# Attention: summing both halves of the older block behind all four heads' scores in the middle slots of a group

## The chip, the cores and the metric

The kernel runs on one core of one Trainium2 chip. The time is that of the whole program on the device, in microseconds (us), the median of several runs. Five engines work side by side: TensorE (PE) multiplies matrices, VectorE (DVE), ScalarE (ACT) and GpSimd (POOL) do the rest, and SyncE (SP) issues transfers. PEld is the loading of weights into TensorE.

## The reference

The input is 2048 tokens of 256 features. Two macaron layers follow one another; each is half a feed-forward network, causal attention with 16 heads of 16 features, and the other half of the feed-forward network, every one behind a layer norm:

```
x = x + 0.5 * ffn0(ln(x));  x = x + attn0(ln(x));  x = x + 0.5 * ffn0(ln(x))
x = x + 0.5 * ffn1(ln(x));  x = x + attn1(ln(x));  x = x + 0.5 * ffn1(ln(x))

q, k, v = heads(x @ W_qkv)                       # 16 heads, 16 features each
s = q @ k.T / 4 (+ position bias in layer 0, rotary q and k in layer 1), masked where key > query
y = softmax(s) @ v;  out = y @ W_o
```

ffn0 has ternary weights and an RMS norm; ffn1 keeps the two largest of each four hidden values. The change touches attention alone, in both layers.

## The kernel before

**Tiling.** Tokens are cut into four chunks c = 0 to 3 of 512 queries (CH), the 16 heads into four quartets g. A group n = 4c + g is one chunk of queries with one quartet of heads, so there are 16 groups per layer. The keys that a group may see are cut into blocks kb of 128 keys, 4(c + 1) of them; T = 4 is the number of blocks in a chunk. A pair (n, kb) is a slot. A layer has 160 slots (16 in c = 0, 32 in c = 1, 48 in c = 2, 64 in c = 3), and `slots` lists them in order (line 833).

**Work of a slot.** For its own block the slot forms the scores of four heads, keys on partitions, in two pairs: `st_pair` (line 725, matmuls at line 733, output `pst`) for heads 2 and 3 (hp = 1) and then heads 0 and 1 (hp = 0). A pair takes two PSUM banks, from a pool of two such pairs. `exp_pair` (line 746, ScalarE, line 753) turns each pair into `pT` in SBUF, which has five buffers. Softmax needs the maximum of every query's scores beforehand, so beside this the slot works ahead for a later group: a "unit" (n, t, kc) of `mx_unit` (line 663) forms, for each of four heads, the scores of 128 queries against 512 keys (matmul `pq`, line 671) and VectorE reduces each to a maximum (`mx`, line 682). A `pq` takes one PSUM bank from a pool of three, `ps_one`. The banks go round, so the fourth `pq` of a unit takes the bank of the first and waits until VectorE has read it. The list `maxima` says which units belong to which slot; slots of groups 0 to 14 with kb <= cT have at least one, and those of the last group have none.

**Sums.** `av_part` (line 759, matmul at line 768, output `pav`) multiplies an older block's `pT` with the values and adds into one PSUM bank `acc` for the whole group. The bank holds the four heads in four strips of 32 partitions, and the work is split into two halves of the query columns, part 0 and part 1. One part of a block with 512 columns is four matmuls of 32 weight columns x 256, one per head; they are f32, and the trace shows two records for each, so eight. Blocks wait for their sums in the deque `unsummed`; `sums(i, part)` (line 929) sums everything up to that part of slot i's block.

**Order.** The order of the instructions on PE, VectorE, ScalarE and GpSimd is that of the Python code; nothing reorders it. In a slot i with a unit (lines 949 to 954) it is: scores of heads 2 and 3, maxima of heads 0 and 1, exponentials, part 1 of block i - 2; then scores of heads 0 and 1, maxima of heads 2 and 3, exponentials, part 0 of block i - 1. In a slot without a unit (lines 955 to 964) both score pairs come first and then both parts of block i - 1. Behind that come the other units of the slot, what has fallen due (`run_due`: turning maxima, the output projection at line 809), and one step of preparing the next chunk (`prep_qk`, `prep_v`) or of a layer norm. Loads of q and k are issued on SP three slots ahead (`load_to(i + 3)`).

Of the kernel before, what the change touches and what calls it, by code (L numbers as in the profile page):

```python
# [31 lines left out]
T = CH // P  # L32
# [14 lines left out]
def macaron_kernel(ctx: ExitStack, tc: tile.TileContext, a, out):  # L47
# [139 lines left out]
    def draw(work):  # L187
        while work and next(work[0], "end") == "end":
            work.popleft()

    def pull():

        for work in list(background)[:2]:
            if next(work, "end") == "end":
                background.remove(work)
# [294 lines left out]
    def attention(layer, following):  # L490
# [9 lines left out]
        with ExitStack() as st:  # L500
# [91 lines left out]
            def prep_v(c):  # L592
                ready(c)
                for t in range(0, T, 2):
                    pp = ps_one(f"pv{layer}_{c}_{t}").rearrange("p (t f) -> p t f", t=2)
                    for i in range(2):
                        for dc in range(DC):
                            nc.tensor.matmul(  # L598
                                pp[:, i, :],
                                lhsT=xns[c][:, dc, (t + i) * P : (t + i + 1) * P],  # L600
                                rhs=wqkv[:, dc, 2 * E : 3 * E],
                                start=dc == 0,
                                stop=dc == DC - 1,
                            )
                    for i in range(2):
                        vs = va[c][:, t + i, 0 : H * VW].rearrange("p (h d) -> p h d", d=VW)[:, :, 0:D]
                        pv = pp[:, i, :].rearrange("p (h d) -> p h d", d=D)
                        if layer == 0:
                            nc.scalar.copy(vs, pv)
                        else:  # L610
                            nc.vector.tensor_tensor(
                                vs, pv, b_v.rearrange("p (h d) -> p h d", d=D), ALU.add
                            )
                    if t + 2 == T:
                        done.add(("v", c))
                    yield
# [108 lines left out]
            def st_pair(n, kb, hp, apart=False):  # L725

                c, g = divmod(n, G)
                kc, t = divmod(kb, T)
                lo = t * P if kc == c else 0
                pair, ps = banks(f"pst{layer}_{n}_{kb}_{hp}", apart)  # L730
                for i in range(2):
                    hh = 2 * hp + i
                    nc.tensor.matmul(  # L733
                        ps[i][:, lo:CH],
                        lhsT=ks[n, kc][0:rows, hh, t * P : (t + 1) * P],
                        rhs=qs[n][0:rows, hh, lo:CH],
                        start=True,
                        stop=kc < c,
                    )
                    if kc == c:  # L740
                        nc.tensor.matmul(  # L741
                            ps[i][:, lo : lo + P], lhsT=ident_b, rhs=mask_kq, start=False, stop=True
                        )
                return pair, ps

            def exp_pair(n, kb, hp, scores):
                pair, ps = scores
                c, g = divmod(n, G)
                kc, t = divmod(kb, T)
                lo = t * P if kc == c else 0  # L750
                pT = ap.tile([P, 2, CH], F32, tag="pT", bufs=5, name=f"pT{layer}_{n}_{kb}_{hp}")
                if pair is not None:
                    nc.scalar.activation(pT[:, :, lo:CH], pair[:, :, lo:CH], AF.Exp, scale=0.25)  # L753
                else:
                    for i in range(2):
                        nc.scalar.activation(pT[:, i, lo:CH], ps[i][:, lo:CH], AF.Exp, scale=0.25)
                return pT

            def av_part(n, kb, pTs, part):
                c, g = divmod(n, G)  # L760
                kc, t = divmod(kb, T)
                lo = t * P if kc == c else 0
                mid = (lo + CH) // 2 if CH - lo > CH // 2 else CH
                a, b = ((lo, mid), (mid, CH))[part]
                if a < b:
                    for hh in range(4):
                        v0 = (4 * g + hh) * VW
                        nc.tensor.matmul(  # L768
                            acc[hh * SLOT : (hh + 1) * SLOT, a:b],
                            lhsT=va[kc][:, t, v0 : v0 + SLOT],  # L770
                            rhs=pTs[hh // 2][:, hh % 2, a:b],
                            start=kb == 0 and part == 0,
                            stop=kb == (c + 1) * T - 1,
                            skip_group_check=True,
                        )
                if part == 0 and kc == c:
                    divide(n, t)
# [89 lines left out]
            def run_due(all_of=False):  # L867
                while True:
                    due = [x for x in later if all_of or x[0] <= now[0]]
                    if not due:  # L870
                        return
                    later.remove(due[0])
                    due[0][1](*due[0][2])
# [3 lines left out]
            def step():  # L877
                draw(preps)

            def need(*what):  # L880
                while what not in done:
                    assert preps, what
                    step()
# [6 lines left out]
            def mx_next(unit, heads):  # L890
                n, t, kc = unit
                mx_unit(n, t, kc, heads)
                if 3 in heads:
                    left[n] -= 1
                    if not left[n]:
                        mx_end(n)
                        at(1, mx_turn, n)
# [8 lines left out]
            def load_to(slot):  # L906
                while uses and uses[0][1] <= slot:
                    load(*uses.popleft()[0])
# [12 lines left out]
            def turned(n):  # L921
                if n % 2 == 1:
                    c, q = divmod(n // 2, G // 2)
                    at(2, turn_back, c, q)
                    if q == G // 2 - 1:
                        for dc in range(DC):
                            at(3 + dc, output, c, dc)

            def sums(i, part):

                while unsummed and unsummed[0][::2] <= (i, part):
                    _, unit, p = unsummed.popleft()
                    n, kb, _ = unit
                    need("v", kb // T)
                    av_part(*unit, p)
                    if p == 1 and kb == (n // G + 1) * T - 1:
                        turned(n)

            for i, (n, kb) in enumerate(slots):
                c = n // G  # L940
                if kb == 0 and n % G == 0 and 0 < c < NCH - 1:

                    preps.extend((prep_qk(c + 1, "k"), prep_qk(c + 1, "q"), prep_v(c + 1)))
                if n not in turned_max:
                    run_due(all_of=True)
                load_to(i + 3)
                units = maxima.get(i, [])
                pTs = [None, None]
                if units:
                    for hp in (1, 0):  # L950
                        ps = st_pair(n, kb, hp)
                        mx_next(units[0], (2 - 2 * hp, 3 - 2 * hp))
                        pTs[hp] = exp_pair(n, kb, hp, ps)
                        sums(i - 2 + (hp == 0), hp)
                else:


                    both = []
                    for hp in (1, 0):
                        both.append(st_pair(n, kb, hp, pairs[0] % 3 == 2))  # L960
                        pairs[0] += 1
                    for hp, ps in zip((1, 0), both):
                        pTs[hp] = exp_pair(n, kb, hp, ps)
                    sums(i - 1, 1)
                unsummed.extend((i, (n, kb, pTs), part) for part in range(2))
                for unit in units[1:]:
                    mx_next(unit, (0, 1, 2, 3))
                run_due()
                if preps and (c <= 1 or i % 2):
                    step()  # L970
                    if c == 0 and i % 2:
                        draw(background)
                else:
                    pull()
                now[0] += 1
# [37 lines left out]
    def begin(layer, following):  # L1013
        att = attention(layer, following)
        begun[:] = att, next(att)
# [149 lines left out]
```

## Time and profile before

| | us |
|---|---|
| median of three runs | 1952.8 (1952.1 to 1952.8) |
| profiled execution | 1957.7 |
| its span, first to last instruction | 1955.7 |
| PE busy | 1761.4 (90% of the span) |
| DVE busy | 1361.6 (70%) |
| ACT busy | 894.2 (46%) |
| POOL busy | 458.4 (23%) |
| attention of layer 0 | about 267 to 787 of the span, PE busy 499.6 of 521 |
| attention of layer 1 | about 1203 to 1764, PE busy 517.1 of 561 |

A timeline row gives start, length, engine, line, operation, output<-inputs, shape and how many instructions were merged; brackets hold the idle time of the engine before it and what ended it. Matmuls are pipelined: one of 512 columns is shown some 0.38 us long, while the next starts 0.22 us later. So on PE the distance between starts is what counts, not the length of a row.

### The profile page before, as it was taken

What the parts mean: (1) busy time and instruction counts of PE and PEld (TensorE: products, weight loads), DVE (VectorE), ACT (ScalarE), POOL (GpSimd) and SP (SyncE); (2) the same over time, 40 slices, a digit from 0 to 9 for tenths busy, and PEclk for the clock granted to TensorE, in tenths of its full rate; (3) what the DMA queues carried; (4) which work ended last, traced back from release to release, by engine and by line L of the source; (5) the groups of instructions that cost most, each with busy time, mean ns of one, the idle gap of its engine ahead of it and who ended that gap; (6) DMA issues with size and microseconds to landing.
All of it is one profiled execution on the core that took longest, in us unless ns stands there. A gap on an engine that the chain in (4) does not pass through costs nothing. (4 is left out here: it accounts for less than half of the span.)

```text
span 1955.7 us, 26994 instructions
## 1 busy us (share of the span) xinstructions
PE 1761.4 (90%) x10684; PEld 726.5 (37%) x10684; DVE 1361.6 (70%) x2384; ACT 894.2 (46%) x1112; POOL 458.4 (23%) x418
## 2 busy tenths in 40 slices
PE   5699789999999999789999876898999999998997
PEld 1233344433433333333444333433333333333443
DVE  7866377787788883666575655868877888825664
ACT  4343254555555668334422312445555656673220
POOL 3455321101000000455453432211111000003422
PEclk9799899999999999989999986999999999999999
DMA  4000252213211000200000115222122110000000
GB/s 129 1 1 33 82 148 83 73 54 102 62 45 46 28 28 2 73 1 0 1 11 0 54 61 158 82 73 92 52 69 86 43 43 26 18 1 0 11 11 22
DMA packets 50510, 93.10 MB, mean 48 GB/s; under 512 B 5424, under 2 KB 33072, under 8 KB 50128
## 3 DMA queue, kind: packets, MB, share of 16 engines
q1 hardware_dynamic: 49296, 89.28, 14.8%
q10 hardware_dynamic: 1088, 2.10, 0.3%
q8 instruction: 84, 1.38, 0.3%
q14 instruction: 42, 0.34, 0.1%
HBM read 59.51 MB, written 27.26 MB: 44 GB/s over the span
## 5 line engine op out<-in xcount | busy, mean ns | idle before, releaser
L682 DVE TENSOR_REDUCE mx<-pq 128x1 f32<-128x512 f32 (+3 forms) x1280 | 708.6, 603 | 158.5 <-PE pq L679 91.2
L753 ACT ACTIVATE pT<-pst 128x1024 f32<-128x1024 f32 (+3 forms) x614 | 542.6, 896 | 334.9 <-PE pst L733 196.8
L671 PE MATMUL pq<-k,q 105*128 105x512 bf16 (+7 forms) x1280 | 378.8, 353 | 74.7 <-DVE mx L682 52.3
L733 PE MATMUL pst<-q,k 99*128 99x512 bf16 (+7 forms) x1280 | 357.7, 354 | 5.1 <-ACT pT L753 4.2
L768 PE MATMUL pav<-pT,va 128*32 128x256 f32 (+1 forms) x4608 | 352.4, 382 | 5.2 <-DVE yt L789 5.0
L281 PE MATMUL pg_f<-xn,wgu 128*128 128x512 f32 x512 | 229.8, 602 | 11.5 <-DVE hr_f L318 11.5
L794 POOL TENSOR_TENSOR zt<-yt,rd 128x64 f32<-128x64 f32 x128 | 38.4, 300 | 795.2 <-DVE rd L793 795.1
L733 PEld LDWEIGHTS <-k 105*128 105x128 bf16 (+1 forms) x1280 | 101.5, 98 | 254.1 <-issue 218.4
L317 ACT ACTIVATE sl_f<-pg_f 128x512 f32<-128x512 f32 x128 | 76.0, 594 | 251.8 <-PE pg_f L281 175.0
L671 PEld LDWEIGHTS <-q 105*128 105x128 bf16 (+1 forms) x1280 | 124.5, 100 | 148.0 <-issue 44.3
L306 PE MATMUL pg_f<-xn,wgu 128*128 128x512 bf16 x512 | 156.2, 413 | 19.5 <-DVE wgu L170 6.8
L768 PEld LDWEIGHTS pav<-pT,va 128*32 128x32 f32 x4608 | 93.8, 108 | 208.7 <-issue 174.8
L281 PEld LDWEIGHTS pg_f<-xn,wgu 128*128 128x128 f32 x512 | 98.6, 193 | 136.9 <-issue 121.0
L306 PEld LDWEIGHTS <-wgu 128*128 128x128 bf16 x768 | 77.7, 101 | 166.9 <-issue 74.7
L292 PE MATMUL po_f<-h_f,wd 128*128 128x512 f32 x256 | 116.3, 608 | 17.3 <-DVE h_f L418 17.3
L340 POOL TENSOR_TENSOR ss_f<-ss_f,sq_f 128x512 f32<-128x512 f32 x56 | 91.1, 1628 | 111.5 <-ACT sq_f L339 111.3
L679 PE MATMUL pq<-mask_qk,ident_b 128*128 128x128 bf16 x512 | 107.3, 227 | 0.0
L741 PE MATMUL pst<-mask_kq,ident_b 128*128 128x128 bf16 x512 | 103.1, 222 | 0.0
L306 PE MATMUL pg_f<-xm_f,wgu 128*128 128x512 bf16 x256 | 85.3, 416 | 14.0 <-DVE xm_f L238 14.0
L318 DVE TENSOR_TENSOR h_f<-sl_f,pg_f 128x512 f32<-128x512 f32 x64 | 43.6, 682 | 76.4 <-ACT sl_f L317 76.3
L789 DVE STREAM_TRANSPOSE yt<-pav 128x128 f32<-128x128 f32 x128 | 39.8, 311 | 76.7 <-PE pav L768 76.7
L394 DVE TENSOR_TENSOR ge_f<-h_f 128x1536 bf16<-128x1536 f32 (+2 forms) x48 | 67.6, 1437 | 28.0 <-ACT h_f L387 28.0
(132 smaller groups left out, 1802.5 us busy)
## 6 DMA issues: line engine op xcount, KB each, us to landing
k<-dk SPq DMA_DIRECT2D x80, 384.0 KB
dk<-p_k SPq DMA_DIRECT2D x48, 256.0 KB
dq<-p_q SPq DMA_DIRECT2D x48, 256.0 KB
q<-dq SPq DMA_DIRECT2D x32, 384.0 KB
x<-in_xT ACTq DMA_DIRECT2D x4, 512.0 KB
raw<-in_w_gu SPq DMA_DIRECT2D x8, 256.0 KB
wgu<-in_w_gu SPq DMA_DIRECT2D x1, 2048.0 KB
cs_k<-in_cos_sin SPq DMA_DIRECT2D x4, 512.0 KB
```

What stands on the lines that cost most here:

```text
L281: nc.tensor.matmul(pg[:, half, :], lhsT=wgu[:, dc, half * F + f * P : half * F + (f + 1) * P], rhs=xn[:, dc, :], start=dc == 0, stop=dc == ...
L292: nc.tensor.matmul(po, lhsT=w[:, f, dc * P : (dc + 1) * P], rhs=h[:, f, :], start=f == 0, stop=f == FC - 1,)
L306: nc.tensor.matmul(pg[:, half, :], lhsT=wgu0[:, dc, half * F + f * P : half * F + (f + 1) * P], rhs=xp[part][:, dc, :], start=part == 0 an ...
L317: nc.scalar.activation(sl, pg[:, 0, :], AF.Silu)
L340: nc.gpsimd.tensor_tensor(ss, ss, sq, ALU.add)
L671: nc.tensor.matmul(pq, lhsT=qs[n][0:rows, hh, t * P : (t + 1) * P], rhs=ks[n, kc][0:rows, hh, 0:w], start=True, stop=kc < c,)
L679: nc.tensor.matmul(pq[:, w - P : w], lhsT=ident_b, rhs=mask_qk, start=False, stop=True)
L682: nc.vector.tensor_reduce(mxs[n][:, t, hh, kc : kc + 1], pq, AX.X, ALU.max)
L733: nc.tensor.matmul(ps[i][:, lo:CH], lhsT=ks[n, kc][0:rows, hh, t * P : (t + 1) * P], rhs=qs[n][0:rows, hh, lo:CH], start=True, stop=kc < c,)
L741: nc.tensor.matmul(ps[i][:, lo : lo + P], lhsT=ident_b, rhs=mask_kq, start=False, stop=True)
L753: nc.scalar.activation(pT[:, :, lo:CH], pair[:, :, lo:CH], AF.Exp, scale=0.25)
L768: nc.tensor.matmul(acc[hh * SLOT : (hh + 1) * SLOT, a:b], lhsT=va[kc][:, t, v0 : v0 + SLOT], rhs=pTs[hh // 2][:, hh % 2, a:b], start=kb == ...
```

## The change

In a slot that has a unit and whose block lies in the middle of its group (1 < kb < cT - 1), the two half sums between the score pairs are left out. In their place both parts of block i - 1 are summed behind the scores and maxima of all four heads. At kb = 2, the first such slot, `sums(i - 1, 1)` finds part 1 of block i - 2 still open and sums three parts; at kb = cT - 1, the first slot behind, half by half again, the first call finds nothing and the second sums part 0 alone. The condition holds for kb = 2 in c = 1, kb = 2 to 6 in c = 2 and kb = 2 to 10 in c = 3 (groups 12 to 14), 51 slots per layer. All instructions stay the same in number and shape on every engine; their order on PE changes.

```diff
                 if units:
+                    full = 1 < kb < c * T - 1
                     for hp in (1, 0):
                         ps = st_pair(n, kb, hp)
                         mx_next(units[0], (2 - 2 * hp, 3 - 2 * hp))
                         pTs[hp] = exp_pair(n, kb, hp, ps)
-                        sums(i - 2 + (hp == 0), hp)
+                        if not full:
+                            sums(i - 2 + (hp == 0), hp)
+                    if full:
+                        sums(i - 1, 1)
                 else:
```

## The prediction

> **What bounds the kernel now.** I read the page first (PE is busy 90% of the span, VectorE 70%, ScalarE 46%), then the timeline of one slot in chunk 3, where nothing else runs beside it:
>
> ```profile
> 643.06 0.61 PE L733 MATMUL pst<-q,k 105*128 105x512 bf16 x2
> 643.50 0.59 PE L671 MATMUL pq<-k,q 105*128 105x512 bf16 x2
> 643.92 1.29 DVE L682 TENSOR_REDUCE mx<-pq 128x1 f32<-128x512 f32 x2 [0.25 <-PE pq L671]
> 644.03 0.64 PE L768 MATMUL pav<-pT,va 128*32 128x256 f32 x8
> 644.60 0.61 PE L733 MATMUL pst<-q,k 105*128 105x512 bf16 x2
> 645.04 0.59 PE L671 MATMUL pq<-k,q 105*128 105x512 bf16 x2
> 645.57 0.64 PE L768 MATMUL pav<-pT,va 128*32 128x256 f32 x8
> 646.14 0.60 PE L733 MATMUL pst<-q,k 105*128 105x512 bf16 x2
> ```
>
> PE waits for nothing here (no bracket), VectorE waits for PE. A half takes 1.54 us, a slot 3.08, and 80 of the 102 slots in which the condition holds start the next slot 3.07 or 3.08 us later. So PE sets the pace and what counts is the distance between its starts. Two scores take 0.44, two `pq` 0.53 up to the sum, the sum 0.57 up to the next scores.
>
> How much of that is the switch between bf16 scores and column-tiled f32 sums? The last group, without units, sums both parts in one run (timeline, three rows of PE):
>
> ```profile
> 758.16 1.04 PE L733 MATMUL pst<-q,k 105*128 105x512 bf16 x4
> 759.31 1.07 PE L768 MATMUL pav<-pT,va 128*32 128x256 f32 x16
> 760.32 1.04 PE L733 MATMUL pst<-q,k 105*128 105x512 bf16 x4
> ```
>
> Sixteen records take 1.07 where eight take 0.64, so eight more take 0.43: two waves of four heads, 0.215 each. Four scores last 1.04 and two 0.61, so a score too takes 0.215. A half is four bf16 matmuls and two waves, 6 x 0.215 = 1.29. The rest of its 1.54 us, 0.25, is paid once for each run of sums: 0.09 ahead of it (0.53 instead of 0.44), 0.13 behind (0.57 instead of 0.44), some 0.03 inside. From start to start the run of sixteen takes 1.01 and not 2 x 0.57, which confirms it. I use 0.245, since eight slots take 24.62 us and not 24.64.
>
> The order that the change makes is already there once, at kb = 0 and 1 of chunk 3, where part 1 of a group's last block is empty and the first half has no sum (timeline, PE and DVE):
>
> ```profile
> 662.86 0.59 PE L671 MATMUL pq<-k,q 105*128 105x512 bf16 x2
> 663.28 2.48 DVE L682 TENSOR_REDUCE mx<-pq 128x1 f32<-128x512 f32 x4 [0.19 <-PE pq L671]
> 663.29 0.59 PE L733 MATMUL pst<-q,k 105*128 105x512 bf16 x2
> 663.73 0.67 PE L671 MATMUL pq<-k,q 105*128 105x512 bf16 x2
> ...
> 665.99 0.38 PE L671 MATMUL pq<-k,q 105*128 105x512 bf16 x1
> ...
> 666.83 0.38 PE L671 MATMUL pq<-k,q 105*128 105x512 bf16 x1 [0.46 <-DVE mx L682]
> ```
>
> With VectorE free (kb = 0) the second pair of `pq` lasts 0.67 instead of 0.59: the fourth waits 0.08 for the first one's bank. With VectorE behind (kb = 1) it waits 0.46.
>
> **The change, part by part.** *Switches.* In PE's order there are 540 runs of sums before and 416 after. 124 fewer: per layer two in each of the four groups of chunk 1, six in each of chunk 2, ten in each of groups 12 to 14 (the slots kb = 2 to cT - 2, and kb = cT - 1, which keeps one run). At 0.245 on the path, -30.4 us. The waves themselves only move: kb = 2 has six, kb = cT - 1 two, the others four.
>
> *The bank of the fourth `pq`.* Until now a sum and a switch lay between the second and the third `pq`, and the first bank was long free. Now the fourth `pq` waits, and behind it on PE's queue the run of sums and all the rest. Bounds: 0 (no bracket in today's halves) and 0.46 (kb = 1). I take the 0.08 of kb = 0. Its cause reads off the rows: the first maximum starts 0.42 behind its `pq`, lasts 0.69, its release reaches PE 0.05 later, at 1.16 behind the first `pq`; PE would be there at 1.08. Whether VectorE stays free: a new slot takes 12 x 0.215 + 0.245 + 0.08 = 2.91, four maxima take 2.48, so 0.4 remain. In the shortest slot (kb = cT - 1, two waves, 2.48) they just fit. 124 x 0.08 = +9.9 us.
>
> *Maxima that are late already.* A delay of VectorE that a half hid (between first and fourth `pq` there were 1.76 us) now stands on the path. Going along the timeline through the 124 slots, I noted how much later than 0.42 (0.47 in a masked unit) the first maximum starts behind its `pq`. In most it does not. The rest:
>
> ```profile
> 453.92 0.59 PE L671 MATMUL pq<-k,q 105*128 105x512 bf16 x2
> ...
> 454.30 0.69 DVE L545 TENSOR_TENSOR dn_k<-pp_k,p_k 128x512 f32<-128x512 f32 x1 [1.77 <-ACT p_k L544]
> 454.91 2.47 DVE L682 TENSOR_REDUCE mx<-pq 128x1 f32<-128x512 f32 x4
> ```
>
> Five slots of layer 0 have L545 ahead, 0.56 to 0.62 each, 2.9 together: it hangs on a projection just before the slot and stays as late. Six have the turned sums (L804), 0.29 each; five the maxima's end (L689, L694), 0.26 to 0.52, 1.8 together; one L571, 0.74; two more a layer norm, 0.52 together, and L819 makes 0.1. That is 7.8 in all. In eleven of these VectorE's queue is the reason and the slot before is changed too; its last maximum then starts 0.70 instead of 0.52 before the next slot's `pq`, which takes off 0.18 each, 2.0. I take +5.8; bounds 0, if other waits cover it, and 11.6, twice that, if the tight slots push the delay on.
>
> *Layer 1, group 5, kb = 2.* There PE waits for VectorE's preparation today; its one switch, 0.2, is not won.
>
> *Exponentials.* `pT` has five buffers. At kb = 2 the second exponential needs the buffer of block 0, whose part 1 is now summed at the slot's end: first part of the run, through at about 2.6 behind the slot's start. The exponential (1.02) then ends near 3.7 instead of 2.6. The slot lasts 14 x 0.215 + 0.245 + 0.08 = 3.34, the next one's first exponential starts at about 3.98 and its second score pair at 4.2: hidden, by 0.3. In later slots the buffers are free a slot ahead. If that cover is gone, 22 groups pay 0.3 at most, 6.6. ScalarE otherwise has 0.9 of 2.9 us idle.
>
> *Queues.* No transfer moves against its slot: SP's loads stay three slots ahead, now 8.7 us and not 9.2. GpSimd's division at line 794 belongs to blocks from cT on, which are summed half by half as before.
>
> Sum: -30.4 + 9.9 + 5.8 + 0.2 = -14.5 us. In the profiled execution that is 1955.7 - 14.5 = 1941.2 of span, 1943.2 with the 2.0 around it. The median of the runs lies 4.9 below the profiled execution, so 1952.8 - 14.5 = 1938.3.
>
> **The rivals.** *Late maxima cost nothing*, since PE has prep work to do in many of those slots: -20.3, 1932.5. Against it: that work stands ahead of the slot, not behind the wait. 14%.
>
> *Late maxima cost double*, 11.6: -8.7, 1944.1. For it: in the shortest slot VectorE has no idle time left. 12%.
>
> *VectorE becomes the bound* (slower). If the fourth `pq` waits 0.46 as at kb = 1, all 124 runs cost 0.215 more than they save: +26.7, 1979.5. It decides from 0.245 a slot, or 0.20 with the late maxima counted. Against it: at kb = 1 VectorE comes out of a slot of 2.27 us, which is shorter than its four maxima, with two other operations between; the new slots are longer than them. 5%.
>
> *The clock* (slower too). PE would wait briefly 124 times; a stretch with half speed in it is the second of these:
>
> ```profile
> 610.00:670.00 60.00, 59.08 (x476) 21.58 (x476) 49.14 (x94) 35.84 (x40) 1.76 (x6) 1.00 0.12 37
> 822.00:830.00 8.00, 4.76 (x14) 1.64 (x14) 7.12 (x10) 2.93 (x6) 5.70 (x4) 0.79 0.01 2
> ```
>
> (The columns are the length, PE, PEld, DVE, ACT, POOL, granted clock, DMA share, GB/s.) There the clock is short by 8 x 0.21 = 1.7 us. Once in each of the 22 changed groups that is 37 against 14.5 won: +22.9, 1975.7; from nine on it is slower. Against it: the first stretch holds such 0.46 us waits, at kb = 1 of groups 12 and 13, at full clock. 4%. The Trainium skill, "TensorE: Matmul & The Clock Gate", section "A second HAM failure mode: psum-queue depth-cycling", speaks for this rival: short idles between matmul groups that cycle through PSUM banks can make the clock swing. By that rule the time would be near 1975.7; this trace's waits up to 0.46 us, at clock 1.00, do not agree with it.
>
> *Given back*: something other than PE sets the end of each attention, 1952.8. Against it: PE is busy 49.5 of 50 us in many stretches there. 5%.
>
> **How the numbers follow.** My forecast has 60%, its own range 1934 to 1942 (late maxima and ring wait each a little either way). Faster by over 0.2%, 3.9 us, about what a measurement of this kernel can tell from no change: 60 + 14 + 12 = 86%; the same 5%; slower 5 + 4 = 9%. The range 1932 to 1946 takes in the first three cases and leaves out 14%.
>
> **What would show it.** In chunk 3 the new slot lasts 2.91 (switch and ring wait right); rows of PE read four scores and `pq`, then pav x16 with the next scores 1.01 later; the fourth `pq` has a wait of about 0.08 on mx; granted clock 1.00 all through chunk 3. With 2.84 the ring wait is absent, with 3.1 or more VectorE binds. Slots behind L545 should take some 3.5. I am wrong if pav x16 costs more than 1.01 behind a waiting `pq`, if scores wait for the exponentials, or if the last group does not start about 6 us before its 756.9 in layer 0 and layer 1 does not win some 8.5 more.

## The result and the profile after

The changed kernel takes 1939.5 us in the median (1937.8 to 1944.2), the kernel before 1953.4 beside it (1952.1 to 1956.2). The ratio is 0.9933, with a 95% interval from 0.9918 to 0.9947: 13.1 us less, between 10.4 and 16.0, where 14.5 had been forecast.

The timeline of PE and VectorE in the middle slots of chunk 3 after the change, to be set against the first one that the prediction showed (start, length, engine, line, operation, output<-inputs, shape, number merged, idle time ahead):

```profile
663.22 1.50 PE L768 MATMUL pav<-pT,va 128*32 128x256 f32 x24
...
667.57 0.60 PE L733 MATMUL pst<-q,k 105*128 105x512 bf16 x2
668.01 0.59 PE L671 MATMUL pq<-k,q 105*128 105x512 bf16 x2
668.44 0.59 PE L733 MATMUL pst<-q,k 105*128 105x512 bf16 x2
668.88 0.68 PE L671 MATMUL pq<-k,q 105*128 105x512 bf16 x2
669.48 1.07 PE L768 MATMUL pav<-pT,va 128*32 128x256 f32 x16
670.48 0.60 PE L733 MATMUL pst<-q,k 105*128 105x512 bf16 x2
...
668.43 2.48 DVE L682 TENSOR_REDUCE mx<-pq 128x1 f32<-128x512 f32 x4 [0.43 <-PE pq L671]
```

The slot takes 670.48 - 667.57 = 2.91 us; it took 3.08. One run of sixteen sums stands where two of eight stood, and takes 1.00 from its start to the next scores. The second pair of `pq` lasts 0.68 and not 0.59: that is the wait for the first one's bank. VectorE still has 0.43 us of idle time in a slot. At kb = 2 the run has 24 records, three parts. Starts of `pst` read slot by slot give 2.91 or 2.92 in all the undisturbed middle slots of chunk 3 (those into which no other work of PE or VectorE falls), 3.34 or 3.35 at kb = 2 and 2.48 at kb = 11; the arithmetic of the prediction had 2.91, 3.34 and 2.48.

On the page the two lines of `pq` and of the sums read before the change:

```profile
L671 PE MATMUL pq<-k,q 105*128 105x512 bf16 (+7 forms) x1280 | 378.8, 353 | 74.7 <-DVE mx L682 52.3
L768 PE MATMUL pav<-pT,va 128*32 128x256 f32 (+1 forms) x4608 | 352.4, 382 | 5.2 <-DVE yt L789 5.0
```

The engines' busy time and the same two lines read after it:

```profile
PE 1735.6 (90%) x10659; PEld 747.2 (39%) x10684; DVE 1353.1 (70%) x2384; ACT 884.7 (46%) x1112; POOL 456.9 (24%) x418
L671 PE MATMUL pq<-k,q 105*128 105x512 bf16 (+7 forms) x1280 | 386.9, 351 | 76.9 <-DVE mx L682 55.3
L768 PE MATMUL pav<-pT,va 128*32 128x256 f32 (+1 forms) x4608 | 326.2, 379 | 5.2 <-DVE yt L789 5.0
```

The sums are busy 326 us instead of 352: one row of 1.07 stands for two of 0.64, 0.21 less, and for 124 runs fewer that makes 26. The waits of `pq` for VectorE come to 55.3 us and were 52.3. Most of the new wait does not show there: a matmul's row is 0.38 long, so a wait of 0.08 lies under the row ahead of it and only lengthens the merged row.

The profiled execution fell from 1957.7 to 1938.7 us, 19.0, more than the medians. The 124 slots in which the order changes account for 14.5 of it (-1.7 in the 102 middle slots, -12.8 in the 22 slots kb = cT - 1, which lost two waves to kb = 2). The unchanged slots of the two attentions are 8.2 us shorter in sum, and the rest of the program is 3.6 us longer. That is a difference of two executions and no part of the forecast; the granted clock, which over the attentions of layers 0 and 1 was 0.99 and 0.97 before and 1.00 and 0.98 after, may be some of it.

### The profile page after: what moved, and what is told of

Read it like the earlier page. It is cut to its first block, busy times and chain, and to the rows that moved or that the text cites. A ratio compares the mean times of both kernels' runs of the same rounds, so it can differ in the third digit from the quotient of the medians.

```text
span 1936.7 us, 26968 instructions
## 1 busy us (share of the span) xinstructions
PE 1735.6 (90%) x10659; PEld 747.2 (39%) x10684; DVE 1353.1 (70%) x2384; ACT 884.7 (46%) x1112; POOL 456.9 (24%) x418
## 5 line engine op out<-in xcount | busy, mean ns | idle before, releaser
L682 DVE TENSOR_REDUCE mx<-pq 128x1 f32<-128x512 f32 (+3 forms) x1280 | 697.6, 602 | 146.0 <-PE pq L679 86.8
L753 ACT ACTIVATE pT<-pst 128x1024 f32<-128x1024 f32 (+3 forms) x614 | 533.1, 895 | 319.9 <-PE pst L733 166.4
L671 PE MATMUL pq<-k,q 105*128 105x512 bf16 (+7 forms) x1280 | 386.9, 351 | 76.9 <-DVE mx L682 55.3
L768 PE MATMUL pav<-pT,va 128*32 128x256 f32 (+1 forms) x4608 | 326.2, 379 | 5.2 <-DVE yt L789 5.0
L733 PEld LDWEIGHTS <-k 105*128 105x128 bf16 (+1 forms) x1280 | 111.0, 98 | 229.4 <-issue 165.2
L768 PEld LDWEIGHTS pav<-pT,va 128*32 128x32 f32 x4608 | 106.6, 109 | 190.9 <-issue 136.1
```

Of the source, the lines that this page charges most:

```text
L671: nc.tensor.matmul(pq, lhsT=qs[n][0:rows, hh, t * P : (t + 1) * P], rhs=ks[n, kc][0:rows, hh, 0:w], start=True, stop=kc < c,)
L682: nc.vector.tensor_reduce(mxs[n][:, t, hh, kc : kc + 1], pq, AX.X, ALU.max)
L733: nc.tensor.matmul(ps[i][:, lo:CH], lhsT=ks[n, kc][0:rows, hh, t * P : (t + 1) * P], rhs=qs[n][0:rows, hh, lo:CH], start=True, stop=kc < c,)
L768: nc.tensor.matmul(acc[hh * SLOT : (hh + 1) * SLOT, a:b], lhsT=va[kc][:, t, v0 : v0 + SLOT], rhs=pTs[hh // 2][:, hh % 2, a:b], start=kb == ...
```

## The experiments

My theory: each run of column-tiled f32 sums between bf16 scores costs 0.245 us of switching, which the change halves, and the fourth `pq` now pays the wait for VectorE to release the first one's bank, 1.16 us behind the first `pq`'s start. The rival in the first three experiments: the 0.17 won per slot is the whole price of a switch, and the wait for the bank hides beside the switch (the drain, as the expectations call it). What it is in a switch that takes the time (the loading of weights, the tiling or the type) none of the runs separates. In the first three, the lines shown go into the slots for which `full` holds; the others keep their order. In all runs the kernel before ran on the same chip.

**The wait made longer.** Both score pairs first, then all four maxima in a row:

```diff
+                    if full:
+                        for hp in (1, 0):
+                            ps = st_pair(n, kb, hp)
+                            pTs[hp] = exp_pair(n, kb, hp, ps)
+                        mx_next(units[0], (0, 1, 2, 3))
+                        sums(i - 1, 1)
```

> In the 102 middle slots both score pairs come first, then all four maxima in a row, then the run of sums; the number of runs of sums stays that of the changed kernel. My theory (a switch costs 0.245 us for each run, and the fourth pq waits until 1.16 us behind the first one's start, when VectorE has released its bank): the fourth pq reaches its turn 3 x 0.215 = 0.65 behind the first instead of 1.08, waits 0.51 instead of 0.08, and the slot in chunk 3 lasts 3.34 instead of 2.91. That is 102 x 0.43 = 44 us over the changed kernel, so about 30 us slower than the kernel before, some 1.5%. Rival (the wait for the bank hides beside the drain ahead of the sums, and the whole gain of 0.17 a slot is the price of the switch itself): the slot stays at 2.91 and the time within 3 us of the changed kernel's, 0.7% faster than before.

Measured: 1981.3 us, ratio 1.0131 (1.0109 to 1.0154), 26 us slower than before, where 30 had been expected. The timeline of PE and VectorE in chunk 3:

```profile
736.01 1.04 PE L733 MATMUL pst<-q,k 105*128 105x512 bf16 x4
736.88 0.81 PE L671 MATMUL pq<-k,q 105*128 105x512 bf16 x3
737.30 2.48 DVE L682 TENSOR_REDUCE mx<-pq 128x1 f32<-128x512 f32 x4 [0.86 <-PE pq L671]
738.04 0.38 PE L671 MATMUL pq<-k,q 105*128 105x512 bf16 x1 [0.35 <-DVE mx L682]
738.35 1.07 PE L768 MATMUL pav<-pT,va 128*32 128x256 f32 x16
739.35 0.82 PE L733 MATMUL pst<-q,k 105*128 105x512 bf16 x3
```

The fourth `pq` starts 738.04 - 736.88 = 1.16 behind the first, as in the changed kernel, although its turn comes at 0.65. The slot takes 739.35 - 736.01 = 3.34, as the theory had it. The 102 middle slots are 39.8 us longer in sum than in the changed kernel and not 44, because some in which VectorE is late anyway take as long in both (5.72 at kb = 2 of group 4, layer 0). VectorE has more idle time than before (0.86): it is its latency on one bank, not its load, that PE waits for.

**The wait taken away.** Both score pairs first again, then three maxima, the run of sums, and the fourth maximum behind it:

```diff
+                        mx_next(units[0], (0, 1, 2))
+                        sums(i - 1, 1)
+                        mx_next(units[0], (3,))
```

> In the 102 middle slots both score pairs come first, then three maxima, the run of sums, and the fourth maximum behind it; as many runs of sums as in the changed kernel. My theory: no pq waits for a bank any more (the fourth comes 1.75 us behind the first, and the next slot's third, which takes its bank, 1.5 us behind the fourth, against 1.16 needed), so the slot in chunk 3 lasts 12 x 0.215 + 0.245 = 2.83 instead of 2.91. That is 102 x 0.08 = 8 us, and of the late maxima the 4.7 us that lie in these slots hide as well: 13 us under the changed kernel, 27 under the kernel before, ratio 0.986. Rival (the wait hides beside the drain): slot 2.91, ratio 0.993.

Measured: 1931.7 us, ratio 0.9887 (0.9871 to 0.9902). The timeline of PE in chunk 3:

```profile
713.20 1.03 PE L733 MATMUL pst<-q,k 105*128 105x512 bf16 x4
714.06 0.81 PE L671 MATMUL pq<-k,q 105*128 105x512 bf16 x3
714.80 1.07 PE L768 MATMUL pav<-pT,va 128*32 128x256 f32 x16
715.80 0.39 PE L671 MATMUL pq<-k,q 105*128 105x512 bf16 x1
716.03 1.03 PE L733 MATMUL pst<-q,k 105*128 105x512 bf16 x4
```

The slot takes 2.83, exactly the waves and one switch. The sum over the 102 middle slots is 12.6 us under the changed kernel's, 2.1 of them in one disturbed slot of layer 1 (below). But of the 13 us forecast, only 8 to 9 arrived. Part of the difference shows in the slots kb = cT - 1, which are 2.4 us longer in sum than in the changed kernel, all of it in four of the 22: they come half by half and without a sum in the first half, and VectorE, which got the fourth maximum late, is late in them. The largest, 1.02 us, is in layer 1, group 9, where the maxima's end (L689, L694) stands ahead of them as well (timeline of PE and VectorE):

```profile
1468.30 0.20 DVE L689 TENSOR_REDUCE neg<-mx 128x16 f32<-128x48 f32 x1
1468.54 0.39 DVE L694 TENSOR_TENSOR neg<-neg 128x16 f32<-128x16 f32 x2
1468.84 2.48 DVE L682 TENSOR_REDUCE mx<-pq 128x1 f32<-128x512 f32 x4
1469.58 0.38 PE L671 MATMUL pq<-k,q 99*128 99x512 bf16 x1 [0.84 <-DVE mx L682]
```

**The switch alone, with the wait kept.** Two runs of sums again, but not between the second and third `pq`:

```diff
+                        for hp in (1, 0):
+                            ps = st_pair(n, kb, hp)
+                            if hp == 1:
+                                sums(i - 2, 1)
+                            mx_next(units[0], (2 - 2 * hp, 3 - 2 * hp))
+                            pTs[hp] = exp_pair(n, kb, hp, ps)
+                        sums(i - 1, 0)
```

> In the 102 middle slots the four heads' maxima come as in the changed kernel, with the second score pair alone between the second and third, but the sums are in two runs again: part 1 of block i - 2 behind the first score pair, part 0 of block i - 1 at the end. Runs of sums as many as before the change (540), the wait for the bank as in the changed kernel. My theory: the slot in chunk 3 lasts 12 x 0.215 + 2 x 0.245 + 0.08 = 3.15, that is 0.24 over the changed kernel and 0.07 over the kernel before; with the late maxima in these slots, 102 x 0.08 + 4.7 = 13 us slower than before, ratio 1.0065. Rival (the price of a switch is 0.165 and the wait for the bank is free): slot 3.08 and the time of the kernel before.

Measured: 1963.4 us, ratio 1.0047 (1.0031 to 1.0064): slower than before by 9 us (13 expected), with as many runs of sums. The timeline of PE in chunk 3:

```profile
729.43 0.61 PE L733 MATMUL pst<-q,k 105*128 105x512 bf16 x2
729.96 0.64 PE L768 MATMUL pav<-pT,va 128*32 128x256 f32 x8
730.53 0.60 PE L671 MATMUL pq<-k,q 105*128 105x512 bf16 x2
730.98 0.59 PE L733 MATMUL pst<-q,k 105*128 105x512 bf16 x2
731.41 0.67 PE L671 MATMUL pq<-k,q 105*128 105x512 bf16 x2
732.01 0.64 PE L768 MATMUL pav<-pT,va 128*32 128x256 f32 x8
732.58 0.60 PE L733 MATMUL pst<-q,k 105*128 105x512 bf16 x2
```

The slot takes 3.15: one more switch than the changed kernel's, +0.24, and the same long pair of `pq`, 0.67. The three runs together separate the terms: without the wait 2.83, with it 2.91, with it and a second switch 3.15. The rival falls.

**Cover for a late VectorE.** One more VectorE instruction, an addition whose result nobody reads, ahead of the first maximum in each middle slot, in the kernel before and in the changed one:

```diff
                         ps = st_pair(n, kb, hp)
+                        if hp == 1 and 1 < kb < c * T - 1:
+                            nc.vector.tensor_tensor(extra, xns[c][:, 0, :], xns[c][:, 1, :], ALU.add)
                         mx_next(units[0], (2 - 2 * hp, 3 - 2 * hp))
```

> The kernel before with one more VectorE instruction (an addition of 128x512 f32 whose result nobody reads) ahead of the first maximum in each of the 102 middle slots; some 0.69 us by L545, 0.62 from start to start. My theory (a late VectorE is hidden by the halves as long as the first maximum is less than 0.59 us late and VectorE's own work fits): it has 4 x 0.60 + 0.62 = 3.03 us of work in a slot of 3.08, so the slot stays at 3.08 and the time within 3 us of the kernel before. Rival (VectorE's lateness costs the old order as much as the new one): 102 x 0.15 or more, 15 us slower than before.

> The changed kernel with the same added instruction in the same 102 slots. My theory: the first maximum comes 0.2 late, the fourth pq waits so much longer, and since VectorE's 3.03 us no longer fit into 2.91, VectorE sets the pace: slot in chunk 3 at 3.03 to 3.10, that is 0.12 to 0.19 over the changed kernel, 12 to 19 us, and the gain over the kernel before is gone (ratio 0.999 to 1.003). Rival (lateness of VectorE is as well hidden as before): 2.91 and the time of the changed kernel, ratio 0.993.

Measured: the kernel before with it 1963.5, ratio 1.0043 (1.0026 to 1.0059), 8 us by the ratio; the changed kernel with it 1968.3, ratio 1.0061 (1.0040 to 1.0081), some 25 us over the changed kernel by the ratios and 29 by the medians. Both cost more than I expected. In chunk 3 the undisturbed slots do nearly as the theory says. In the kernel before they stay at 3.08 (timeline of PE and VectorE, from a slot's second half to the next one's):

```profile
731.16 0.60 PE L733 MATMUL pst<-q,k 105*128 105x512 bf16 x2
...
733.30 0.68 DVE L954 TENSOR_TENSOR extra<-xn 128x512 bf16<-128x512 f32 x1
733.90 2.48 DVE L682 TENSOR_REDUCE mx<-pq 128x1 f32<-128x512 f32 x4
734.24 0.61 PE L733 MATMUL pst<-q,k 105*128 105x512 bf16 x2
```

In the changed one VectorE works without a pause and sets the pace at 734.95 - 731.96 = 2.99, a little less than the 3.03 expected:

```profile
731.96 0.61 PE L733 MATMUL pst<-q,k 105*128 105x512 bf16 x2
732.31 0.68 DVE L957 TENSOR_TENSOR extra<-xn 128x512 bf16<-128x512 f32 x1
732.90 2.48 DVE L682 TENSOR_REDUCE mx<-pq 128x1 f32<-128x512 f32 x4
...
734.95 0.61 PE L733 MATMUL pst<-q,k 105*128 105x512 bf16 x2
```

What I had left out are the slots in which VectorE is late anyway. In the kernel before, 15 of the 102 slots, most of them behind L545 or L804, pay 0.33 to 0.88 us each for the added instruction: the half's cover of about 0.6 is used up there, and more lateness goes through in full. Behind L804, for one, the first maximum was 0.29 late; with 0.62 more it is 0.91 late, and 0.34 of it is paid. In two slots of layer 1 (groups 8 and 9) the added instruction itself takes 1.56 and 1.79 us and not 0.68, beside a product on GpSimd (L575). In the changed kernel 36 slots pay 0.5 us or more, and every kb = 2 of chunk 3 is among them with 0.51 or 0.52 (0.00 in the kernel before): VectorE comes late out of kb = 1 there. So the halves cover about 0.6 us of lateness in a slot without masks and no more, and the new order has lost that cover.

**A wider version.** The order with the fourth maximum behind the sums, also at kb = 1 and kb = cT - 1:

```diff
-                    full = 1 < kb < c * T - 1
+                    full = 0 < kb < c * T
```

> The order of the run with the fourth maximum behind the sums, also in slots kb = 1 and kb = cT - 1 of chunks 1 to 3; 394 runs of sums instead of 416. My theory: 22 x 0.245 = 5.4 us for the runs, 22 x 0.08 = 1.8 for the bank in slots kb = cT - 1 and 1 for late maxima there, and at kb = 1 the sums fill the wait for VectorE (0.46 in chunk 3, some 0.33 in chunks 1 and 2, 8 us in all, if VectorE catches up in the slots behind, where it has 0.4 us a slot to spare): 8 to 16 us under the narrower order, ratio to the kernel before about 0.98. Rival (VectorE's arrears at kb = 0 and 1 are only handed on and PE waits for them later): 8 us under it, and the wait shows at kb = 2 instead.

Measured: 1921.3 us (1915.1 to 1922.9), ratio 0.9827 (0.9804 to 0.9849), the fastest of all, 10 us under the narrower order. The timeline of PE and VectorE at kb = 1 of group 13, layer 0:

```profile
648.85 1.04 PE L733 MATMUL pst<-q,k 105*128 105x512 bf16 x4
649.72 0.81 PE L671 MATMUL pq<-k,q 105*128 105x512 bf16 x3
...
650.27 1.85 DVE L682 TENSOR_REDUCE mx<-pq 128x1 f32<-128x512 f32 x3
650.46 1.07 PE L768 MATMUL pav<-pT,va 128*32 128x256 f32 x16
651.47 0.39 PE L671 MATMUL pq<-k,q 105*128 105x512 bf16 x1
```

VectorE is late as it was before the change (its first maximum starts 1.42 behind the slot's start, 1.43 before), but the sums stand ahead of the fourth `pq` and nothing waits. All slots from kb = 1 to 11 of this group take 2.83 or 2.84; kb = 1 took 3.02, and kb = 12, whose first half has no sum now, takes 2.87 instead of 3.56. VectorE's arrears do not come back at kb = 2 in chunk 3, so the rival falls there. In chunks 1 and 2 kb = 2 takes 2.83 or 2.84 too in ten of the sixteen groups; in the other six VectorE has other work, and the two are not told apart.

## Why the prediction was right

*What bounds it.* PE in the middle slots; right: the slot follows PE's arithmetic to 0.01 us in four orders (2.83, 2.91, 3.15, 3.34). Before the change 78 of the 102 slots read 3.07 or 3.08 and two 3.06; the prediction counted 80.

*Switches, -30.4 us.* Right: 0.24 a run by the third experiment against the changed kernel, and the last group's rows had shown it before. Eight slots in 24.62 us and waves of 0.215 give 0.249 and not 0.245, which is 0.5 us in 124 runs and changes nothing.

*The bank of the fourth `pq`, +9.9 us.* Right: 0.08 a slot by the second experiment, and 1.16 behind the first `pq` by the first. The rows of kb = 0 were the nearest ones, and the 0.46 of kb = 1 belonged to a VectorE that was behind. That 0.46 was read too low, though: it is PE's idle time, while the 0.08 is a distance of starts. By the starts that the prediction shows, the fourth `pq` of kb = 1 comes 666.83 - 665.99 = 0.84 behind the third and so 0.62 late. The rival in which all 124 runs wait as at kb = 1 should have cost 124 x (0.62 - 0.245) = 46 us and not 26.7.

*Late maxima, +5.8 us.* Right in kind, but half as much again as was measured: the 124 slots exceed what the switches, the waves and the bank make of them by 3.8 us in sum, group 5 of layer 1 left out. The largest are the five slots behind L545, in which the first maximum waits as forecast (2.8 us together, 2.9 forecast). Chunk 2, group 8, kb = 2 after the change (timeline of PE and VectorE):

```profile
452.74 0.59 PE L671 MATMUL pq<-k,q 105*128 105x512 bf16 x2
453.12 0.69 DVE L545 TENSOR_TENSOR dn_k<-pp_k,p_k 128x512 f32<-128x512 f32 x1 [1.77 <-ACT p_k L544]
...
454.46 0.38 PE L671 MATMUL pq<-k,q 105*128 105x512 bf16 x1 [0.22 <-DVE mx L682]
454.77 1.50 PE L768 MATMUL pav<-pT,va 128*32 128x256 f32 x24
456.20 0.60 PE L733 MATMUL pst<-q,k 105*128 105x512 bf16 x2
```

That slot takes 3.90, which is 0.56 over 3.34. The excess of the others came out smaller: behind L804 a slot takes 2.99, 0.08 more (0.11 forecast), behind L689 and L694 in chunk 2 some 0.04 more in three of four. Masked units do not even pay the 0.08: with their masks the turn of the fourth `pq` comes 1.26 behind the first (group 10, kb = 5, layer 0), and the bank is free at 0.48 + 0.69 + 0.05 = 1.22.

*Layer 1, group 5, kb = 2: 0.2 not won.* Wrong by 2.0 us: the slot takes 9.81 where it took 7.35, and two more waves and the 0.2 would have made it 7.8. VectorE's preparation (L577, L579) still stands ahead of the maxima. The granted clock in the slot was 0.58 and had been 0.83: in both executions the first two scores take 1.03 us or more there instead of 0.60, but now the run of sums is still slow, with 2.79 us for 24 records that take 1.50 elsewhere. The first experiment took 9.89 there at a clock of 0.57, the second 7.67 at 0.67 and the third 7.48 at 0.66. So the slot is slow in both orders that have the fourth `pq` right ahead of one long run, and not in the two others; but how much of it is the order and how much the clock was not separated.

*The sum, -14.5 us.* Partly luck: the late maxima came out 2.0 us lower than forecast and that one slot 2.0 us higher, so that the 124 slots sum to the forecast. What the record bears out is the two terms for the switch and the bank.

*Exponentials hidden by 0.3.* Right. ScalarE's timeline at kb = 2 and 3 of group 13, layer 0:

```profile
661.96 1.02 ACT L753 ACTIVATE pT<-pst 128x1024 f32<-128x1024 f32 x1 [1.07 <-PE pst L733]
663.95 1.02 ACT L753 ACTIVATE pT<-pst 128x1024 f32<-128x1024 f32 x1 [0.98 <-PE pav L768]
665.30 1.95 ACT L753 ACTIVATE pT<-pst 128x1024 f32<-128x1024 f32 x2 [0.32 <-PE pst L733]
```

The second exponential waits for the run of sums (pav), ends at 664.97, and the next slot's scores are 0.32 later.

*The rivals.* Nothing was given back: the last group of layer 0 starts 9.6 us earlier (747.23 for 756.85) and that of layer 1 another 10.6, where the prediction had named about 6 and 8.5 as the sign. That is more than the forecast, as this execution was 19.0 us shorter in all. VectorE did not become the bound; its pace with four maxima and 0.6 us more is 2.99, so it would decide only with some 0.5 us of further work in a slot. The clock did not swing: through chunk 3 after the change (a stretch; length, busy PE, PEld, DVE, ACT, POOL, granted clock, DMA share, GB/s) it is full.

```profile
604.00:747.00 143.00, 140.62 (x1232) 57.86 (x1228) 116.57 (x225) 89.46 (x104) 3.80 (x13) 1.00 0.10 29
```

The Trainium skill, "TensorE: Matmul & The Clock Gate", section "A second HAM failure mode: psum-queue depth-cycling", tells of a kernel in which short idles between matmul groups made the clock swing; with waits of 0.08 us here, and of 0.5 us in the first experiment, whose chunk 3 ran at clock 1.00 too, it did not. Late maxima were neither free nor twice as dear.

## What to carry to other kernels

Where an engine changes between two kinds of instruction, look for a place in the same trace where it does so half as often, and read the price from the distance of starts. Before moving work out of the space between two instructions, ask which buffer's release that work was hiding: here a third of what the switches gave went back to a bank that is released 1.16 us after it was taken, and putting one `pq` behind the sums brought most of it back. An order that takes out slack also takes out the cover for every other engine's lateness, so the same lateness is dearer afterwards.

## What was not expected

An added VectorE instruction cost the old order 8 us, in 15 of 102 slots, although VectorE had idle time in an average slot: cover is a limit in each slot (about 0.6 us here), not a mean. And the waits of `pq` for VectorE rose by only 3 us on the page, while 0.08 in each of the 102 middle slots alone is 8 us: waits shorter than the 0.17 us by which matmul rows overlap do not appear as idle time.
